# Position taps of the second pass in halves of two rows, two taps scaled by ScalarE and summed by transfers, queries of two groups in quarters

## The chip, the cores and the metric

The kernel runs on one core of a Trainium2 chip. The metric is the device time of one execution in microseconds (us), the median of several runs. The engines are named as in the profile: PE (TensorE, matmuls), PEld (its weight loads), DVE (VectorE), ACT (ScalarE), POOL (GpSimd) and SP (SyncE, which here only issues transfers).

## What is computed

The input x has 4 images of 192 channels and 128 x 128 pixels, in float32. Two layers follow one another:

```python
# layer 0: 1x1 convolution to q, k, v, l, a 3x3 convolution of each channel,
# attention between the 24 channels of a head, a gate from l, projection
# layer 1:
pe = depthwise_conv3x3(x, pos_w)                       # padding 1
x = x + pe + pos_b
q, k, v = split(einsum('oc,bchw->bohw', qkv_w, x))     # three groups of 64 channels each
for dil in (1, 2, 3):                                  # one group each, two heads of 32 channels
    # each pixel attends to the 3x3 pixels around it at distance dil (reflected at the edges)
    scores = sum_d(q * k_at_9_pixels) / sqrt(32); a = softmax(scores); o = sum_9(a * v_at_9_pixels)
out = einsum('oc,bchw->bohw', proj_w, concatenate(o))
```

The change lies in layer 1, in the step `x + pe + pos_b` and in the product that makes q.

## The kernel before, in words

Three stages run one after the other: `project` (1x1 and 3x3 convolutions of layer 0), `channel_attention`, and `second_pass`, which holds the end of layer 0 and all of layer 1. The second pass treats two images at a time in blocks of RB = 4 rows (512 pixels): 64 blocks, n = 0 to 63, the first 32 for images 0 and 1. A block goes through these steps.

- **h**: transfers load x and the values of layer 0 (`loads`, SP's queue, buffers `xv`); PE multiplies (`h_product`, L870), ACT adds the gate and writes the rows into rings of 12 rows (`h_evict`, L874). Channels 0 to 127 of the two images lie side by side in `hboth`; channels 128 to 191 of both images share the partitions of a third ring.
- **y**, the nine position taps, for channels 0 to 127 of two images, 1024 elements in each of 128 partitions: ACT starts the sum in PSUM with the centre tap and the bias (`centre`, L910), seven taps follow on DVE, each a multiply and add into the same sum (`tap`, L922; the last writes to y in SBUF). ACT scales the ninth tap (`moved`, L934) and POOL adds it (`moved_sum`, L939). For channels 128 to 191, ACT scales all nine taps (`side`, L946), two accumulating transfers that POOL issues sum rows of three taps (`side_rows`, L958), and POOL adds the remaining three (`side_sum`, L966 and L969).
- **k, v**: PE multiplies y (`kv_product`, L1009, L1012), ACT copies the result into rings (`kv_evict`, L1022).
- **q and scores**: `query` makes q of one group in a PSUM bank: two products of 64 columns for y's first 128 channels (L1069), one full product for the rest (L1066). DVE multiplies q with three shifted windows of k at a time (`prod`, L1077, nine a block), PE sums over a head's channels (`pick_sums`, L1088).
- **softmax**: a transposing product by a constant `order` (L1137), then DVE, ACT and POOL in turn (L1140 to L1170), and a transposing transfer.
- **output**: PE spreads each weight over its channels (`expand`, L1210, 27 a block), DVE multiplies with a window of v (`term`, L1216, 27 a block), POOL sums them (`term_sum`, L1219, 24 a block), PE projects (`out_product`, L1228, L1232), ACT evicts and SP stores.

**What sets the order.** Each step is added to a planner (`Schedule.add`) with its engine, a rank, a cost in us, and the steps that it comes after. The planner plays the steps through: whenever an engine is free, it takes the step of lowest rank of those ready, and writes down the order. A change of tiling mode on PE is charged, and counts against a step's rank. The instructions are issued in this order, and each engine works through its own list in order. A rank is n plus a number of the table `PLACES`, plus a step for each repeat. Buffers take part: `hold` makes the first step of a use wait for the last step of the use that had the buffer before. [...] `pc` 2, `ex` 2, `q` 1, `sc` 1, and `pa`, the sum of the taps, one buffer of two banks.

Of the kernel before, what the change touches and what calls it, by code (L numbers as in the profile page):

```python
# [9 lines left out]
AF = mybir.ActivationFunctionType  # L10
# [176 lines left out]
def rows3(t):  # L187
    return t.rearrange("p (r w) -> p r w", w=W)


FULL, COLS, ROWS, QUADS = "128x128", "128x64", "64x128", "128x32"
HALVES = [slice(0, G), slice(G, 128)]
EXTRA = 2 * B * CH0 + B
SM = EXTRA + B * 2 * CH0
XV = 8
GATE = "wl wl2 dwl fc1T bfc1 fc2T bfc2 eye wprojT".split()
SECOND = "wp1 wq1 wq2 wkv wkv2 wo wo2 posw posb pick order spread".split()
AROUND = (0, 1, 2, 6, 7, 8, 3, 5)

PLACES = {
    "loads": (2.4009, 0),
    "h_product0": (2.3439, 0),
    "h_evict0": (-1.2020, 0),
    "h_product1": (2.8426, 0),
    "h_evict1": (9.5243, 0),
    "h_product2": (3.0534, 0),
    "h_evict2": (3.3755, 0),  # L210
    "centre": (3.2944, 0),
    "tap": (4.7047, 0),
    "moved": (5.7274, 0),
    "moved_sum0": (8.4467, 0),
    "side1": (2.5636, 0.00009),
    "side0": (4.2983, 0.34214),
    "side_rows0": (4.7711, 0),
    "side2": (4.3133, 0),
    "side_rows2": (4.5576, 0),
    "side_sum1": (12.0962, 0),  # L220
    "side_sum2": (7.0378, 0),
    "kv0": (5.2031, 0),
    "kvev0": (3.8148, 0),
    "kv1": (6.4619, 0),
    "kvev1": (8.5235, 0.00001),
    "kv2": (6.0990, 0.18519),
    "kvev2": (5.9292, 0),
    "query0": (6.1573, 0.00001),
    "prod0": (6.9366, 0.00008),
    "query1": (6.5060, 0),  # L230
    "prod1": (7.1376, 0),
    "query2": (7.1323, 0.00003),
    "prod2": (7.5724, 0.00451),
    "pick0": (4.7039, 0.95999),
    "pick1": (15.4739, 0),
    "evicted_scores": (8.2142, 0),
    "by_pixel": (4.8132, 0),
    "top": (9.2303, 0),
    "below": (13.5404, 0),
    "exponential": (4.7718, 0),  # L240
    "total": (6.8232, 0),
    "divide": (3.7907, 0),
    "part0": (4.5732, 0),
    "rest": (6.0317, 0),
    "part1": (5.9516, 0),
    "part2": (6.6828, 0),
    "weights": (7.4677, 0),
    "expand": (8.0527, 0.03805),
    "term": (7.9973, 0),
    "term_sum": (9.4625, 0.01039),  # L250
    "out0": (9.2437, 0),
    "outev0": (9.1400, 0),
    "store0": (7.8234, 0),
    "out1": (9.4456, 0.00001),
    "outev1": (9.8720, 0),
    "store1": (8.3096, 0),
}

@with_exitstack
# [549 lines left out]
def second_pass(tc, x, w2, xv_p, mix1, mix2, biases, v_dram, v2_dram, out):  # L809
# [4 lines left out]
    with ExitStack() as ctx:  # L814
# [5 lines left out]
            dict(  # L820
                xv=XV, y=3, y2=3, prod=4, middle=2, side=1, moved=1, term=4, acc=4, o=3, s_sb=1, e=2, mx=2, sm=2, e_sb=2,
            ),
            dict(pc=2, ex=2, q=1, pa=1, sc=1),
            dict(xv=xv_p),
            (0.12, 0.4177),
        )
        add, hold, tile_of, tiles = stage.schedule.add, stage.hold, stage.tile, stage.tiles
        fill, read, repeat, written = stage.fill, stage.read, stage.repeat, stage.written
# [14 lines left out]
        def at(name, n, k=0):  # L843
            first, step = PLACES[name]
            return n + first + step * k
# [57 lines left out]


        by_row = lambda a: a.rearrange("p r b w -> p (r b) w")

        def centre(n):
            at = n * RB % RING
            to, of = tile_of("pa", ("pa", n), (128, RB, 2, W)), hboth[:, at : at + RB, :, 1 : W + 1]
            nc.scalar.activation(  # L910
                by_row(to), by_row(of), AF.Identity, bias=posb[:, 0:1], scale=posw[:, 0, 4:5]
            )

        def tap(n, t, last):

            acc = tiles["pa", n]
            to = tile_of("y", ("y", n), (128, RB, 2, W)) if last else acc
            if last:
                for im in range(2):
                    tiles["y", n, im] = to[:, :, im, :]  # L920
            for at, length, o in runs(n, t // 3 - 1, RING, False):
                nc.vector.scalar_tensor_tensor(  # L922
                    by_row(to[:, o : o + length]),
                    by_row(hboth[:, at : at + length, :, t % 3 : t % 3 + W]),
                    posw[:, 0, t : t + 1],
                    by_row(acc[:, o : o + length]),
                    ALU.mult,
                    ALU.add,
                )

        def moved(n, t):
            to = tile_of("moved", ("moved", n), (128, RB, 2, W))
            at = n * RB % RING
            nc.scalar.activation(  # L934
                by_row(to), by_row(hboth[:, at : at + RB, :, t % 3 : t % 3 + W]), AF.Copy, scale=posw[:, 0, t : t + 1]
            )

        def moved_sum(n):
            nc.gpsimd.tensor_add(tiles["y", n], tiles["y", n], tiles.pop(("moved", n)))  # L939

        def side(n, ty, tx):

# [19 lines left out]
        def side_sum(n, tx):  # L962
# [5 lines left out]
            y = tiles["y", n, 2]  # L968
            nc.gpsimd.tensor_add(y, y, tiles.pop(("side", n, 1))[:, 2, :])  # L969

        def plan_conv(n):
            prev = first = add("ACT", at("centre", n), 1.25, (centre, n), latency=0.3)
            for m in range(2):
                read("h", m, n, 0, first)
            for j, t in enumerate(AROUND[:7]):
                prev = add("DVE", at("tap", n, j), 1.19, (tap, n, t, j == 6), [prev])
                for m in range(2):
                    read("h", m, n, t // 3 - 1, prev)
            hold("pa", first, prev)
            two = prev  # L980
            mv = add("ACT", at("moved", n), 1.2, (moved, n, AROUND[7]))
            for m in range(2):
                read("h", m, n, 0, mv)
            both = add("POOL", at("moved_sum0", n), 2.39, (moved_sum, n), [mv, two])
            hold("moved", mv, both)
            firsts, sums = {}, []
            for j, ty in enumerate((1, 0, 2)):
                for tx in range(3):
                    sd = add("ACT", at(f"side{ty}", n, tx), 0.72, (side, n, ty, tx), firsts.get(ty, [])[-1:])
                    read("h", 2, n, ty - 1, sd)  # L990
                    firsts.setdefault(ty, []).append(sd)
                if j:
                    after = [firsts[1][-1], firsts[ty][-1], *sums[-1:]]
                    sums.append(add("POOL", at(f"side_rows{ty}", n), 0.9, (side_rows, n, ty), after, latency=6.0))
                    hold("side", firsts[ty][0], sums[-1])
            for tx in (1, 2):
                sums.append(add("POOL", at(f"side_sum{tx}", n), 1.26, (side_sum, n, tx), sums[-1:]))
            hold("middle", firsts[1][0], sums[-1])
            return [sums[-2], two, both, [both, sums[-1]]]


        def kv_product(n, pair, j):
# [16 lines left out]
        def kv_evict(n, pair, im, e, kind, g):  # L1019

            _, _, rows, pad = ring_rows(n, kind, g)
            nc.scalar.copy(rows[HALVES[im], :, pad : pad + W], rows3(tiles["pkv", n, pair, im])[HALVES[e]])  # L1022

        def reflect(n, kind, g):
            _, _, rows, pad = ring_rows(n, kind, g)
# [33 lines left out]
            for at, length, o in runs(n, dy, size, True):  # L1059
                yield ring[g][:, at : at + length, dx : dx + W], slice(o * W, (o + length) * W)  # L1060

        def query(n, g, j):

            q = tile_of("q", ("q", n, g)) if j == 0 else tiles["q", n, g]
            if j:
                mm(q, wq2[:, g, :], tiles["y", n, 2], start=False, stop=True)  # L1066
                return
            for im in range(2):
                mm(rows3(q[HALVES[im]]), wq1[:, g * G : (g + 1) * G], tiles["y", n, im], start=True, stop=False)  # L1069

        def prod(n, g, ty):

# [22 lines left out]

        def plan_scores(n, y):
            prods, used, picks = [], [], []
            for g in range(NG):
                a = add("PE", at(f"query{g}", n), 1.0, (query, n, g, 0), [y[2]], COLS)
                b = add("PE", at(f"query{g}", n, 1), 0.86, (query, n, g, 1), [a] + y[3], FULL)  # L1100
                used += [a, b]
                mine = []
                for ty in range(3):
                    op = add("DVE", at(f"prod{g}", n, ty), 1.67, (prod, n, g, ty), [b])
                    read("k", g, n, (ty - 1) * (g + 1), op)
                    mine.append(op)
                hold("q", a, *mine)
                prods += mine
            for row in range(7):
                of = prods[4 * row // 3 : min(4 * row + 3, NG * NT - 1) // 3 + 1]  # L1110
                op = add("PE", at(f"pick{row % 2 * (row < 6)}", n, row // 2), 0.86, (pick_sums, n, row), of, QUADS)
                op["after"] += picks[-1:]
                picks.append(op)
            for k, op in enumerate(prods):
                hold("prod", op, picks[(3 * k + 2) // 4])
            return used, picks
# [183 lines left out]
def _shapes_only():  # L1300
# [6 lines left out]
    pick[np.arange(128), QR + np.arange(128) // HD1] = 1  # L1307
    order = np.zeros((128, NS), f)
    for col in range(NS):
        order[col // 4 % 4 * 32 + col // 16 * 4 + col % 4, col] = 1  # L1310
    spread = np.zeros((3, NT, 4, NT, 4, HD1), f)
    for t in range(NT):
        for h in range(4):
# [117 lines left out]
```

## Time and profile before

| | |
|---|---|
| median of 3 runs | 4451.89 us (4449.25 to 4452.1) |
| profiled execution | 4448.27 us |
| its span, first to last instruction | 4446.5 us |
| instructions | 64145 |
| mean granted TensorE clock | 0.987 of full speed |
| busy share of the span: PE, DVE, ACT, POOL | 98%, 87%, 57%, 75% |
| transfers | 608.93 MB, of it 99.89 MB on the queue of POOL |
| first centre tap of the second pass | 1644.3 us |
| last tap | starts at 4254.8 us |

A row of the profile names the line of the kernel, the engine, the operation, what it writes and reads (buffer numbers left out), the shape as partitions x elements, and the number of instructions; behind the first bar stand the busy time in us and the mean length of one in ns, behind the second the idle time before them and what ended it. [...] what an instruction costs is read from its start to the next start. In the rows of waits, the first name had to wait for the second: us in total, times, longest.

### The profile page before, as it was taken

The page shows a single profiled execution, that of the slowest core. Times are in us where ns is not written, and L with a number is a line of the kernel's source. Part 1 is how long each engine was busy: PE and PEld are TensorE (multiplying, and loading weights), DVE is VectorE, ACT ScalarE, POOL GpSimd, SP SyncE. Part 2 cuts the span into 40 slices and gives each one's busy share as a digit, 9 for nine tenths or more (in the row PEclk, how much of TensorE's full clock was granted, in tenths as well). Part 3 has the DMA queues.
Part 4 walks back from the last instruction along what each step waited for, and adds up shares of the span by engine and source line. Part 5 has one row for each costly group of instructions (what it writes and reads, how often), then busy time and mean ns, then how long its engine had stood idle before and what let it go on. Part 6 is the DMA issues. An engine that isn't in the chain of part 4 may idle for free.

```text
span 4446.5 us, 64145 instructions
## 1 busy us (share of the span) xinstructions
PE 4340.2 (98%) x20608; PEld 1632.8 (37%) x20608; DVE 3875.7 (87%) x5556; ACT 2523.0 (57%) x4794; POOL 3350.1 (75%) x3343
## 2 busy tenths in 40 slices
PE   9999999899999998999999999999999999999996
PEld 3333333354455542333333333333333333333321
DVE  7998888855555546999999999999999999999996
ACT  7888888733333336555556555555555555555531
POOL 6787777711211113999999999999999999999998
PEclk9999999999999999999999999999999999999997
DMA  8777787678876744444444444444444444443411
GB/s 270 243 246 230 239 255 245 197 163 177 181 170 141 172 104 114 109 98 107 103 104 103 100 103 111 104 100 102 96 104 104 99 111 99 110 105 93 98 36 32
DMA packets 483951, 608.93 MB, mean 137 GB/s; under 512 B 136528, under 2 KB 318364, under 8 KB 483616
## 3 DMA queue, kind: packets, MB, share of 16 engines
q1 hardware_dynamic: 464160, 504.94, 42.0%
q0 software_dynamic: 19456, 99.89, 11.4%
q8 instruction: 166, 2.72, 0.3%
q14 instruction: 169, 1.38, 0.1%
HBM read 277.72 MB, written 201.33 MB: 108 GB/s over the span
## 4 chain that ended last, share of the span: by engine, by line
PE 92%; POOL 3%; DVE 2%; DMA 1%; issue 1%; ACT 1%; SPq 0%; POOLq 0%; DVEq 0%; ACTq 0%
PE pc L638 11%; PE ph L870 11%; PE sc L1088 9%; PE ex L1210 9%; PE pu L355 7%; PE pkv L1009 7%; PE pkv L1012 4%; PE pu L360 4%; PE gram L710 4%; PE q L1069 4%; PE po L1232 4%; PE po L1228 4%; PE q L1066 4%; PE pu L488 2%; POOL acc L1219 2%; PE pu L369 1%
## 5 line engine op out<-in xcount | busy, mean ns | idle before, releaser
L1219 POOL TENSOR_TENSOR acc<-acc,term 128x512 f32<-128x512 f32 x1536 | 1984.4, 1297 | 101.7 <-DVE term L1216 34.4
L1216 DVE TENSOR_TENSOR term<-ex,vring 128x512 f32<-128x512 f32 (+2 forms) x1596 | 1001.9, 666 | 29.2 <-PE ex L1210 18.8
L1077 DVE TENSOR_TENSOR prod<-q,kring 128x1536 f32<-128x1536 f32 (+1 forms) x600 | 1005.7, 1690 | 19.3 <-ACT kring L1027 11.0
L425 POOL TENSOR_TENSOR v_True<-v_True,side 128x512 f32<-128x512 f32 (+1 forms) x512 | 647.8, 1267 | 171.2 <-ACT side L414 143.7
L402 DVE SCALAR_TENSOR_TENSOR pa<-vboth,dwv,pa 128x1024 f32<-128x1024 f32 (+1 forms) x448 | 574.3, 1282 | 78.4 <-ACT pa L395 55.7
L1210 PE MATMUL ex<-e_sb,spread 108*128 108x512 bf16 x1728 | 556.8, 387 | 28.0 <-DVE term L1216 22.1
L922 DVE SCALAR_TENSOR_TENSOR pa<-hboth,posw,pa 128x1024 f32<-128x1024 f32 (+1 forms) x384 | 492.0, 1281 | 34.0 <-ACT pa L910 20.7
L625 POOL COPY band<-band 64x384 f32<-64x384 f32 x192 | 96.6, 503 | 560.9 <-DMA band<-in_bands 392.1
L638 PE MATMUL pc<-u,band 64*64 64x508 f32 (+1 forms) x4608 | 516.9, 590 | 1.5 <-ACT ring L384 1.5
L1088 PE MATMUL sc<-prod,pick 128*32 128x512 f32 x3456 | 475.1, 604 | 2.3 <-DVE prod L1077 1.5
L651 DVE BATCH_NORM_STATS2 stats<-pc 128x6 f32<-128x128 f32 x1440 | 303.3, 284 | 140.8 <-ACT conv L647 140.6
L1009 PE MATMUL pkv<-y,wkv 128*128 128x512 f32 x768 | 371.6, 605 | 11.1 <-ACT vring L1022 10.8
L647 ACT COPY conv<-pc 128x512 f32<-128x512 f32 x384 | 211.5, 587 | 294.7 <-PE pc L638 288.1
L355 PE MATMUL pu<-xt,wx 128*128 128x512 f32 x768 | 366.4, 613 | 8.5 <-DMA xt<-in_x 8.5
L870 PE MATMUL ph<-xv,mix 128*128 128x512 f32 (+1 forms) x1024 | 369.2, 597 | 3.0 <-DMA xv<-v_dram 2.4
L414 ACT ACTIVATE side<-ring,dwv 128x512 f32<-128x512 f32 (+1 forms) x512 | 350.7, 736 | 11.6 <-POOL v_True L425 10.9
L1210 PEld LDWEIGHTS <-spread 108*128 108x128 bf16 x1728 | 130.3, 98 | 610.7 <-issue 592.7
L1022 ACT COPY kring<-pkv 64x512 f32<-64x512 f32 x384 | 223.6, 582 | 228.5 <-PE pkv L1012 223.0
L946 ACT ACTIVATE side<-hring,posw 128x512 f32<-128x512 f32 x512 | 338.6, 708 | 23.6 <-DMA side<-side 11.3
L1022 ACT COPY vring<-pkv 64x512 f32<-64x512 f32 x384 | 224.1, 583 | 136.5 <-PE pkv L1012 118.7
L638 PEld LDWEIGHTS pc<-u,band 64*64 64x64 f32 x4608 | 188.3, 133 | 301.8 <-issue 281.1
L373 ACT COPY us<-pu 128x512 f32<-128x512 f32 x384 | 203.7, 601 | 81.4 <-PE pu L360 81.4
(164 smaller groups left out, 5912.1 us busy)
## 6 DMA issues: line engine op xcount, KB each, us to landing
qk_dram<-us SPq DMA_DIRECT2D x192, 512.0 KB
u<-qk_dram SPq DMA_DIRECT2D x384, 256.0 KB
side<-side POOLq DMA_DIRECT2D x124, 768.0 KB, 6.3
xt<-in_x SPq DMA_DIRECT2D x64, 512.0 KB
v_dram<-v_False SPq DMA_DIRECT2D x64, 512.0 KB
xv<-in_x SPq DMA_DIRECT2D x128, 256.0 KB
xv<-v_dram SPq DMA_DIRECT2D x128, 256.0 KB
out<-o SPq DMA_DIRECT2D x128, 256.0 KB
```

What stands on the lines that cost most here:

```text
L355: mm(pu, wx[:, mt * 128 : (mt + 1) * 128], tiles["xt", n][:, im, :], start=True, stop=False)
L402: nc.vector.scalar_tensor_tensor(by_row(to[:, o : o + length]), by_row(vboth[:, at : at + length, :, t % 3 : t % 3 + W]), dwv[:, 0, t : t ...
L425: nc.gpsimd.tensor_add(v[:, rows, :], v[:, rows, :], z[:, rows, :])
L638: nc.tensor.matmul(pcs[e][r * G : (r + 1) * G, :, to], band[at, e, c, dx, :], u[at, e, c, :].rearrange("p (b w) -> p b w", w=W)[:, :, of], ...
L870: mm(to, w[:, cols], tiles["xv", n, j, im], start=j == 0, stop=j == 2)
L922: nc.vector.scalar_tensor_tensor(by_row(to[:, o : o + length]), by_row(hboth[:, at : at + length, :, t % 3 : t % 3 + W]), posw[:, 0, t : t ...
L1009: mm(rows3(tile_of("pc", key)), w, tiles["y", n, im], start=True, stop=False)
L1077: nc.vector.tensor_mul(to[:, :, px].rearrange("p t (r w) -> p t r w", w=W), q.unsqueeze(1).to_broadcast([128, 3, *q.shape[1:]]), three,)
L1088: mm(sc[quad * 32 : (quad + 1) * 32, :], pick[:, QR - 4 * row : QR - 4 * row + 32], tiles["prod", n, k // NT, k % NT // 3][:, k % 3, :], s ...
L1210: mm(rows3(tile_of("ex", ("ex", n, g, t))), spread[:, t, :], e_sb, start=True, stop=True)
L1216: nc.vector.tensor_mul(rows3(to[:, px]), rows3(ex[:, px]), win)
L1219: nc.gpsimd.tensor_add(tiles["acc", n, g], tiles["acc", n, g], tiles.pop(("term", n, g, t)))
```

## The change

**Position taps.** The sum of the taps now takes one bank: a half of two rows (512 elements) at a time, in the one buffer of `pa`. ACT starts a half (`centre`), DVE adds six taps to it (`tap`, taps 0, 1, 2, 6, 7, 5), then the next half follows. Taps 3 and 8 are both scaled by ACT into one tile (`moved`). Two accumulating transfers, issued by POOL, take the place of POOL's sum: the first adds the two scaled taps, the second adds their sum to y.

**Queries.** `q` has two buffers. The queries of groups 0 and 1 are made together: four products of 64 columns for the first 128 channels, and for the rest four products of 64 x 64, one in each quarter of the array, where there were two full ones. For that, group 1 has its two images in the other halves of the partitions (`place`), in q and in the ring of k, and the constant `order` is changed to match.

**Planner.** Accumulating transfers become two steps: an issue of 0.9 us on POOL and a transfer on an engine "DMA" of its own. All ranks in `PLACES` are new, and a change of tiling mode counts 0.1456 instead of 0.4177 against a rank.

```diff
+SUMMED, MOVED = (0, 1, 2, 6, 7, 5), (3, 8)
...
-    "loads": (2.4009, 0),
+    "loads": (-9.1531, 0),
-    "centre": (3.2944, 0),
-    "tap": (4.7047, 0),
-    "moved": (5.7274, 0),
-    "moved_sum0": (8.4467, 0),
+    "centre0": (1.7649, 0),
+    "tap0": (4.0491, 0),
+    "centre1": (2.2535, 0),
+    "tap1": (0.2255, 0.00005),
+    "moved": (5.4417, 0.00002),
+    "moved_sum0": (-1.3279, 0),
+    "moved_sum1": (2.2850, 0),
-    "prod0": (6.9366, 0.00008),
+    "prod0": (2.7121, 0.00004),
-    "prod2": (7.5724, 0.00451),
+    "prod2": (3.0588, 0.00004),
-    "term": (7.9973, 0),
+    "term": (4.3386, 0),
...
-            dict(pc=2, ex=2, q=1, pa=1, sc=1),
+            dict(pc=2, ex=2, q=2, pa=1, sc=1),
-            (0.12, 0.4177),
+            (0.12, 0.1456),
...
-        def centre(n):
+        place = lambda im, g, kind="k": HALVES[im ^ (g == SWAPPED and kind == "k")]
+        def centre(n, half):
+            at = (n * RB + 2 * half) % RING
+            to, of = tile_of("pa", ("pa", n, half), (128, 2, 2, W)), hboth[:, at : at + 2, :, 1 : W + 1]
...
-        def moved_sum(n):
-            nc.gpsimd.tensor_add(tiles["y", n], tiles["y", n], tiles.pop(("moved", n)))
+        def moved_sum(n, k):
+            reach = runs(n, MOVED[1 - k] // 3 - 1, RING, False)
+            flat = lambda a: a[:, reach[0][2] : reach[-1][2] + reach[-1][1]].rearrange("p r b w -> p (r b w)")
+            of = tiles["moved", n]
+            nc.gpsimd.dma_start(flat(tiles["y", n] if k else of[:, 0]), flat(of[:, 1 - k]), accum_op=ALU.add)
...
+        def summed_by_transfer(rank, us, run, after):
+            issue = add("POOL", rank, 0.9, run, after)
+            return add("DMA", rank + 0.01, us, (lambda: None,), [issue], latency=2.0)
...
-            prev = first = add("ACT", at("centre", n), 1.25, (centre, n), latency=0.3)
-            for j, t in enumerate(AROUND[:7]):
-                prev = add("DVE", at("tap", n, j), 1.19, (tap, n, t, j == 6), [prev])
-            mv = add("ACT", at("moved", n), 1.2, (moved, n, AROUND[7]))
-            both = add("POOL", at("moved_sum0", n), 2.39, (moved_sum, n), [mv, two])
+            for half in range(2):
+                prev = first = add("ACT", at(f"centre{half}", n), 0.68, (centre, n, half), two[-1:], latency=0.3)
+                for j, t in enumerate(SUMMED):
+                    u = at(f"tap{half}", n, j)
+                    prev = add("DVE", u, 0.62, (tap, n, t, half, j == 5), [prev])
+                hold("pa", first, prev)
+                two.append(prev)
+            for k, t in enumerate(MOVED):
+                mvs.append(add("ACT", at("moved", n, k), 1.15, (moved, n, k, t), mvs[-1:]))
+            both = summed_by_transfer(at("moved_sum0", n), 4.0, (moved_sum, n, 0), mvs)
+            both = summed_by_transfer(at("moved_sum1", n), 4.0, (moved_sum, n, 1), [both, two])
...
-                mm(q, wq2[:, g, :], tiles["y", n, 2], start=False, stop=True)
+                        w, of = wq2[HALVES[im], g, HALVES[im]], tiles["y", n, 2][HALVES[im]]
+                        mm(q[place(im, g)], w, of, start=False, stop=True)
...
-            for g in range(NG):
-                a = add("PE", at(f"query{g}", n), 1.0, (query, n, g, 0), [y[2]], COLS)
+            for groups in ((0, 1), (2,)):
+                a = add("PE", at(name, n), 1.0 * len(groups), (query, n, groups, 0), [y[2]], COLS)
+                second = QUARTERS if len(groups) == 2 else FULL
...
-        order[col // 4 % 4 * 32 + col // 16 * 4 + col % 4, col] = 1
+        head = col % 4 ^ 2 * (col // GT == SWAPPED)
+        order[col // 4 % 4 * 32 + col // 16 * 4 + head, col] = 1
```

## The prediction

> **What bounds the kernel now.** I read the page first. Its 40 slices show three stretches; the edit touches only the last one, the second pass, from about 1645 us (first centre tap) to the end. So the next view is the busy time of each engine in stretches of 420 us, ten blocks each, and in what follows the last tap at 4255 us.
>
> ```profile
> core 0: us, PE busy (x) PEld busy (x) DVE busy (x) ACT busy (x) POOL busy (x), PEclk, DMA share, GB/s
> 2100.00:2520.00 420.00, 420.00 (x1731) 144.22 (x1729) 418.96 (x471) 236.70 (x474) 395.85 (x320) 1.00 0.44 104
> 2520.00:2940.00 420.00, 418.37 (x1718) 143.87 (x1720) 416.50 (x468) 237.81 (x477) 395.16 (x319) 1.00 0.43 102
> 4255.00:4446.00 191.00, 149.35 (x537) 45.03 (x533) 142.69 (x203) 37.23 (x85) 167.21 (x135) 0.85 0.13 34
> ```
>
> PE, DVE and POOL all look full. A busy share can't part them, because matmul ends are modelled. Who waits for whom can; these are waits between 2000 and 4000 us (some 47.6 blocks), in us, times and the longest:
>
> ```profile
> PEld q L1069 <- DVE prod L1077: 40.3, 48, 1.1
> PEld sc L1088 <- DVE e L1144: 35.0, 46, 0.8
> POOL acc L1219 <- DVE term L1216: 24.2, 51, 0.7
> DVE term L1216 <- PE ex L1210: 1.4, 3, 0.6
> ```
>
> PE and POOL wait for DVE; DVE hardly waits for anyone. So DVE is the bound, and the sum of its instructions should give the length of a block. The maximum of the softmax runs once a block; ten of them start between 2121.0 and 2499.2 us, so a block takes 378.2/9 = **42.02 us**.
>
> ```profile
> L1140 DVE TENSOR_REDUCE mx<-st x10: 604/621/623, 2121.0 to 2499.2; 128x48 f32<-128x432 f32 x10
> ```
>
> The order of DVE's instructions in time gives what each costs from its start to the next start (first column start, second length of the group):
>
> ```profile
> 3017.14 2.61 DVE L922 SCALAR_TENSOR_TENSOR pa<-hboth,posw,pa 128x1024 f32<-128x1024 f32 x2
> 3019.66 0.68 DVE L1216 TENSOR_TENSOR acc<-ex,vring 128x512 f32<-128x512 f32 x1
> 3020.26 0.68 DVE L1216 TENSOR_TENSOR term<-ex,vring 128x512 f32<-128x512 f32 x1
> 3020.86 1.28 DVE L922 SCALAR_TENSOR_TENSOR pa<-hboth,posw,pa 128x1024 f32<-128x1024 f32 x1
> 3022.05 1.28 DVE L1216 TENSOR_TENSOR term<-ex,vring 128x512 f32<-128x512 f32 x2
> 3023.24 1.75 DVE L1077 TENSOR_TENSOR prod<-q,kring 128x1536 f32<-128x1536 f32 x1
> 3024.91 1.28 DVE L1216 TENSOR_TENSOR term<-ex,vring 128x512 f32<-128x512 f32 x2
> ```
>
> A product costs 1.67 (3023.24 to 3024.91), two terms 1.19 (3022.05 to 3023.24), a tap followed by other work 1.19 (3020.86 to 3022.05). Two taps in a row cost 2.52 (3017.14 to 3019.66), so a tap right behind the one whose sum it reads costs 0.13 more than 1.19: its predecessor has to be written out first. The softmax's four are 0.66 + 0.52 + 0.97 + 0.37 = 2.52 in the same view. Seven taps with on average 0.9 direct followers (57 of 448, counted in the trace) are 7 x 1.19 + 0.9 x 0.13 = 8.45. Block: 27 x 0.595 + 9 x 1.67 + 8.45 + 2.52 = 42.07, against 42.02 measured. The sum closes: **DVE is saturated**, and only its own sum, or a new wait, can move a block.
>
> [...] the tap of a border block, with 768 elements, is 270 ns shorter than one with 1024[...] the trace has 4608 matmuls of 64x64 in 516.9 us, 0.112 each. [...]
>
> **The change, part by part, for a block of four rows.**
>
> *DVE taps.* Seven of 1024 elements go, twelve of 512 come (six for each half). No row shows a 512-element tap, so I extrapolate:
>
> ```profile
> L922 DVE SCALAR_TENSOR_TENSOR pa<-hboth,posw,pa 128x1024 f32<-128x1024 f32 x372 | 479.7, 1290 | 25.3 <-ACT pa L910 12.1 <-ACT hboth L874 7.7 <-ACT hboth L175 2.9
> L922 DVE SCALAR_TENSOR_TENSOR pa<-hboth,posw,pa 128x768 f32<-128x768 f32 x12 | 12.2, 1020 | 8.8 <-ACT pa L910 8.7
> ```
>
> 1290 - 2 x 270 = 750 ns long; less the 0.10 by which a tap overlaps the next instruction (1.29 to 1.19), **0.65 us**, or 0.78 right behind its predecessor. Bounds: 0.60, what the cheapest 512-element operation here (a term) costs, and 0.78. The new planner figure is 0.62 (1.19 for the whole tap before); it has no price for a direct follower. Both rows span two banks, so a cost of crossing a bank, if there is one, would be in my 0.65. With k direct followers a block: 12 x 0.65 + 0.13 k = 7.80 + 0.13 k, against 8.45: **break-even at k = 5**. One tap fewer is worth no more than five extra fixed costs.
>
> *How many followers.* Half 0 has rank n + 4.05, behind most products and near terms (n + 4.34), so it fills gaps; half 1 has n + 0.23. In the kernel before the taps of block n run some 4.7 blocks ahead of the terms and 3 ahead of the products that run beside them (centre of the 31st block at 2821.1, its term work from 3019.7). At a lead of four a term has n - 4 + 4.34 = n + 0.34, behind half 1. So half 1 mostly runs as one burst: 5 followers. Half 0 goes into gaps between pairs of terms, where one whole tap went before and two halves fit: about 2. **k = 7**: 8.71, so +0.26 a block. With 62 of the 64 blocks in the saturated stretch: +16 us.
>
> *ACT.* One centre of 1.21 becomes two of 512 elements (0.7 to 0.8 each, side taps of 512 take 0.71 to 0.80), and one more scaled tap of 1.15 comes: about +1.4 a block. ACT is busy 237 of 420; what hides it is that DVE doesn't wait for ACT now. New wait: the centre of half 1 waits for the last tap of half 0, since one bank is left for these sums. Behind it on ACT stand evictions of h, keys and values; PE and the rings wait for those, and DVE for both. If DVE's order has no other work there, it costs up to a centre and two hand-overs, about 1 us; bounds 0 and 1, I take 0, since terms and products stand ready at most times.
>
> *POOL.* The sum of 1024 elements (2.36, or 2.32 start to start) goes; two accumulating transfers come. One such issue takes 0.61 until the next start and the next sum is 0.3 longer: 0.92. Its block was 24 x 1.277 + 2.32 + 1.23 + 1.24 + 2.85 (softmax) + 2 x 0.92 = 40.1 and becomes 39.7: still under DVE. Both issues wait in POOL's order, the first for the two scaled taps, the second for the first transfer and half 1; queued behind are term sums, and DVE needs their buffers (four terms, 5.1 us of cover). Landing at 512 KB: 576 KB took 5.6 and 768 KB 6.3, so about 5.4, twice in a row; before, the same sum took 2.4. Y is three deep and leads by blocks, so I cost that at nothing in the steady stretch and at 0 to 8 us once at the start.
>
> *DMA.* 128 x 512 KB more, 67 MB. The software queue's 99.9 MB took 11.4%; so 7.7% of the span, 13% of the pass: share 0.44 to 0.57. No bound.
>
> *PE.* The second half of two queries in quarters: eight quarter passes at 0.112 = 0.90 instead of four whole ones (four whole passes of the keys take 1.72 from their start to the next group's, 3018.92 to 3020.64 in PE's order): 1.72. PE gains 0.8 and the second query buffer frees it from waiting for products (40.3 us above). Since DVE waits for PE 1.4 us in 2000, this is worth nothing now: bounds 0 and 0.03 us a block. If the quarters don't overlap, it costs 0.8 on an engine with some 2 us of waits on DVE in each block.
>
> *Order and SP.* All places move. DVE's instructions other than taps are the same in number and size. Loads move to n - 9.15, so SP asks as early as eight buffers allow; a load that waits there holds the stores and the transpose behind it. With DVE the bound, cover is plenty. The stretch after the last tap (191 us, DVE 143 busy, POOL 167) may change by some 10 us either way; I take 0.
>
> *Sum.* The profiled execution took 4448.27 (span 4446.5), the median of the runs is 4451.89, 0.1% more. 4448.3 + 16 = **4464 us**. A measurement of this kernel can tell about 0.2% (9 us) from no change.
>
> **Rivals.** *Interleaved, or cheaper halves* (ends faster). The mechanism: the order puts terms between most taps (k = 3), or a sum in one bank costs the planner's 0.62. k = 3 at 0.65: 8.19, -0.26, so 4432. k = 3 at 0.62: 7.83, -0.62, so 4410. It decides from k below 5 at 0.65, or below 7.8 at 0.62. For it: taps before stand singly; a second query buffer gives DVE more choice. Against: half 1's rank. *A new wait on DVE*: between the halves, or for a term buffer that POOL frees late while it waits for a transfer. At 0.6 us a block on top: 42.9, +53, so about 4500. For it: four issues instead of two on POOL's queue in order, and one bank. Against: DVE waits were 0 in the steady stretch. *No change*: k near 5, or the drain gives back the 16: 4450. *The quarters don't run side by side*: PE is hidden anyway, as above, and the time is the forecast's.
>
> **How the numbers follow.** Forecast 0.46 (its own range 4455 to 4485), faster rival 0.27, new wait 0.17, no change 0.10. The range reaches to 4412 and 4500, leaving out the cheapest end of the faster rival and half of the wait's case. Faster than 4443: the rival and a sliver, 0.28. Within 0.2%: the fourth case and the low end of the forecast, 0.20. Slower: 0.52.
>
> **What would show it.** Half taps some 750 ns long and 0.65 to the next start; more than five a block directly behind one another; mean distance of the softmax maxima near 42.3; DVE without waits; PE and POOL with more waits on DVE. I am wrong if halves are near 0.62 and singled out by terms (41.4 a block), or if DVE shows waits for ACT or POOL in the steady stretch.

## The result, and the profile after

| | before | changed |
|---|---|---|
| median of 12 runs each | 4450.8 us | 4453.06 us |
| ratio to before, 95% interval | | 1.0005, 0.9996 to 1.0014 |
| span of the profiled execution | 4446.5 us | 4451.2 us |
| block of four rows in the steady stretch | 42.02 us | 42.11 us |

The change makes no difference that this measurement can tell. The prediction had the time 11 us too long. It held a slower kernel for likeliest (0.52), which didn't come, and gave this outcome 0.20; its range, 4412 to 4500 us, holds the time.

The rows that answer to those shown of before come from the same views. Busy time of each engine in ten blocks, twice, and after the last taps:

```profile
core 0: us, PE busy (x) PEld busy (x) DVE busy (x) ACT busy (x) POOL busy (x), PEclk, DMA share, GB/s
2100.00:2520.00 420.00, 414.38 (x1765) 137.82 (x1758) 417.54 (x521) 247.25 (x495) 390.22 (x331) 1.00 0.57 127
2520.00:2940.00 420.00, 414.88 (x1770) 138.01 (x1768) 417.14 (x520) 248.83 (x500) 391.80 (x331) 1.00 0.57 128
4255.00:4446.00 191.00, 152.65 (x541) 41.97 (x539) 144.74 (x207) 33.96 (x76) 168.94 (x137) 0.84 0.13 35
```

PE and POOL each have 3.4 to 5.6 us less work in 420, ACT has 10 to 11 more, the DMA share went from 0.44 to 0.57, and DVE is as full as before, with 50 instructions more. The last stretch changed by 2 us on DVE and POOL. The waits say the same:

```profile
POOL acc L1257 <- DVE term L1254: 67.5, 149, 1.5
DVE term L1254 <- PE ex L1248: 0.4, 1, 0.4
```

The second row is the only wait of DVE between 2000 and 4000 us that the view lists. POOL's wait for DVE's terms grew from 24.2 to 67.5: what POOL was spared became idle time. The softmax maxima give the block, (2503.0 - 2124.0)/9 = 42.11 us:

```profile
L1178 DVE TENSOR_REDUCE mx<-st x10: 594/594/598, 2124.0 to 2503.0; 128x48 f32<-128x432 f32 x10
```

The half taps, by shape (busy us, mean ns), and three places of DVE's order in one block of the steady stretch:

```profile
L931 DVE SCALAR_TENSOR_TENSOR pa<-hboth,posw,pa 128x512 f32<-128x512 f32 x630 | 469.8, 746 | 31.6 <-ACT pa L916 24.1
```

```profile
2129.51 0.75 DVE L931 SCALAR_TENSOR_TENSOR pa<-hboth,posw,pa 128x512 f32<-128x512 f32 x1
2130.29 0.75 DVE L931 SCALAR_TENSOR_TENSOR y<-hboth,posw,pa 128x512 f32<-128x512 f32 x1
...
2143.60 1.53 DVE L931 SCALAR_TENSOR_TENSOR pa<-hboth,posw,pa 128x512 f32<-128x512 f32 x2
2145.04 0.68 DVE L1254 TENSOR_TENSOR term<-ex,vring 128x512 f32<-128x512 f32 x1
2145.64 1.75 DVE L1113 TENSOR_TENSOR prod<-q,kring 128x1536 f32<-128x1536 f32 x1
2147.30 2.33 DVE L931 SCALAR_TENSOR_TENSOR pa<-hboth,posw,pa 128x512 f32<-128x512 f32 x3
2149.67 0.75 DVE L931 SCALAR_TENSOR_TENSOR y<-hboth,posw,pa 128x512 f32<-128x512 f32 x1
2150.33 0.68 DVE L1254 TENSOR_TENSOR acc<-ex,vring 128x512 f32<-128x512 f32 x1
...
2161.78 0.74 DVE L931 SCALAR_TENSOR_TENSOR pa<-hboth,posw,pa 128x512 f32<-128x512 f32 x1
2162.43 0.68 DVE L1254 TENSOR_TENSOR term<-ex,vring 128x512 f32<-128x512 f32 x1
2163.03 0.74 DVE L931 SCALAR_TENSOR_TENSOR pa<-hboth,posw,pa 128x512 f32<-128x512 f32 x1
```

The first two rows are the end of a half 0; the next taps are the half 1 behind it, and the last rows begin the next half 0. Half 1 comes almost as the burst that the ranks promised, in a pair and a four with a term and a product between them: four of its taps follow another tap directly, at 0.78 to 0.79 from start to start. Half 0 stands singly between other work, 0.65 to the next start, but for its last two taps. So a block of the steady stretch has 5 direct followers, 4 of half 1 and 1 of half 0. Over the whole pass 338 of 768 taps follow one of the same sum, 5.3 a block; the difference lies at the ends of the pass.

### The profile page after: what moved, and what is told of

The parts are those of the page before. It is cut to its first block, busy times and chain, and to the rows that moved or that the text cites. A ratio compares the mean times of both kernels' runs of the same rounds, so it can differ in the third digit from the quotient of the medians.

```text
span 4451.2 us, 65440 instructions
## 1 busy us (share of the span) xinstructions
PE 4312.1 (97%) x20864; PEld 1594.0 (36%) x20864; DVE 3870.5 (87%) x5876; ACT 2593.4 (58%) x4922; POOL 3320.8 (75%) x3407
## 3 DMA queue, kind: packets, MB, share of 16 engines
q14 instruction: 175, 1.43, 0.1%
## 4 chain that ended last, share of the span: by engine, by line
PE 76%; DVE 14%; issue 6%; POOL 2%; DMA 1%; ACT 1%; SPq 0%; POOLq 0%; DVEq 0%; ACTq 0%
PE pc L642 11%; PE sc L1124 9%; DVE term L1254 8%; PE pu L359 7%; PE pkv L1038 7%; PE ex L1248 7%; PE pkv L1041 4%; PE pu L364 4%; PE ph L874 4%; PE gram L714 4%; PE q L1102 4%; PE po L1270 4%; PE pu L492 2%; DVE pa L931 2%; DVE prod L1113 2%
## 5 line engine op out<-in xcount | busy, mean ns | idle before, releaser
L1257 POOL TENSOR_TENSOR acc<-acc,term 128x512 f32<-128x512 f32 x1536 | 2019.4, 1317 | 167.4 <-DVE term L1254 90.6
L1113 DVE TENSOR_TENSOR prod<-q,kring 128x1536 f32<-128x1536 f32 (+1 forms) x600 | 1001.2, 1681 | 21.3 <-PE q L1105 13.8
L1248 PE MATMUL ex<-e_sb,spread 108*128 108x512 bf16 x1728 | 604.2, 386 | 62.7 <-DVE term L1254 37.7
L931 DVE SCALAR_TENSOR_TENSOR pa<-hboth,posw,pa 128x512 f32<-128x512 f32 (+1 forms) x640 | 474.7, 742 | 39.7 <-ACT pa L916 32.1
L1124 PE MATMUL sc<-prod,pick 128*32 128x512 f32 x3456 | 447.2, 601 | 5.8 <-DVE e L1182 3.2
L874 PE MATMUL ph<-xv,mix 128*128 128x512 f32 (+1 forms) x1024 | 397.4, 602 | 5.3 <-DMA xv<-v_dram 4.7
L1248 PEld LDWEIGHTS <-spread 108*128 108x128 bf16 x1728 | 141.9, 97 | 653.2 <-issue 631.0
L963 ACT ACTIVATE side<-hring,posw 128x512 f32<-128x512 f32 (+1 forms) x512 | 334.4, 708 | 4.8 <-DMA side<-side 2.8
L1273 ACT COPY o<-po 128x512 f32<-128x512 f32 x192 | 106.3, 588 | 276.7 <-PE po L1266 185.9
```

Source lines behind the costliest of these rows:

```text
L874: mm(to, w[:, cols], tiles["xv", n, j, im], start=j == 0, stop=j == 2)
L931: nc.vector.scalar_tensor_tensor(by_row(to[:, o : o + length]), by_row(hboth[:, at : at + length, :, t % 3 : t % 3 + W]), posw[:, 0, t : t ...
L1113: nc.vector.tensor_mul(to[:, :, px].rearrange("p t (r w) -> p t r w", w=W), q.unsqueeze(1).to_broadcast([128, 3, *q.shape[1:]]), three,)
L1124: mm(sc[quad * 32 : (quad + 1) * 32, :], pick[:, QR - 4 * row : QR - 4 * row + 32], tiles["prod", n, k // NT, k % NT // 3][:, k % 3, :], s ...
L1248: mm(rows3(tile_of("ex", ("ex", n, g, t))), spread[:, t, :], e_sb, start=True, stop=True)
L1257: nc.gpsimd.tensor_add(tiles["acc", n, g], tiles["acc", n, g], tiles.pop(("term", n, g, t)))
```

## The experiments

**Theory A**: DVE is saturated; a block is 33.57 us (42.02 - 8.45) plus the taps, and what PE and POOL are spared is hidden. **Rivals**: the halves did free DVE and new waits took it back (B); PE (D) or POOL (E) binds beside DVE; the transfers slow the other engines (F). In each sum below the followers are those of the steady stretch, counted in the kernel's trace. Where an experiment "keeps the order", only what a step issues is changed, not the plan. All ratios are to the kernel before, run beside it on the same chip.

**What PE and POOL were spared is given back.** First the quarters:

```diff
-SWAPPED = 1
+SWAPPED = -1
...
-                if j and len(groups) == 1:
+                if j:
```

> The changed kernel with its order kept, but the second half of the queries of groups 0 and 1 made by two full products each in place of four quarters; the images keep their own halves of the partitions. PE gets about 0.8 us more a block. Theory A: PE's saving was hidden, so giving it back changes the time by less than 9 us. Rival D, PE is a bound beside DVE and the quarters paid for other losses: 30 to 50 us longer.

Measured: 4456.02 us, ratio 1.0010 (1.0002 to 1.0018), 3 us from the changed kernel. PE's busy time between 2100 and 2520 us rose from 414.38 to 418.33, 0.4 a block where 0.8 was expected:

```profile
2100.00:2520.00 420.00, 418.33 (x1722) 142.32 (x1713) 417.28 (x520) 246.57 (x495) 389.71 (x330) 1.00 0.57 128
```

Then the second transfer:

```diff
+            if k:
+                nc.gpsimd.tensor_add(flat(tiles["y", n]), flat(tiles["y", n]), flat(of[:, 0]))
+                return
```

> The changed kernel with its order kept, but the second accumulating transfer is a POOL sum of 1024 elements in the same place: POOL gets about 2.32 - 0.95 = 1.4 us more a block and one transfer fewer. Theory A: POOL has some 3 us of waits a block, so the time changes by less than 9 us. Rival E, POOL is a bound beside DVE: 40 us or more longer. Rival F, the transfers slow DVE, ACT or PE: it gets shorter by more than 9 us.

Measured: 4452.01 us, ratio 1.0001 (0.9993 to 1.0009). POOL's busy time rose by 14.4 us in ten blocks, 1.4 a block, and the block stayed at (2501.6 - 2122.6)/9 = 42.11:

```profile
2100.00:2520.00 420.00, 414.39 (x1766) 137.85 (x1762) 417.55 (x520) 246.89 (x495) 404.65 (x330) 1.00 0.49 115
```

D, E and F fall: both savings were hidden, and giving up one of the two transfers didn't shorten anything. The second query buffer stayed in both kernels; what it alone does was not measured.

**DVE gets less.** One tap is left out of each half:

```diff
         def tap(n, t, half, last):
+            if t == 0:
+                return
```

> The changed kernel with its order kept, and tap 0 left out of both halves (so that tap's part of the sum is missing): two DVE instructions fewer in a block. Theory A, DVE's own sum is the block: it goes by 0.656 in half 0 and 0.656 + 0.127 in the burst of half 1, 1.44 us a block, 62 blocks, down to 89 us less (about 4364), at least 35 us less if another engine binds soon. Rival B, the halves did free DVE and new waits on ACT, POOL or the transfers hold the block at 42.1: the time stays within 9 us of 4453 and DVE gets 1.4 us of waits a block.

Measured: 4402.18 us, ratio 0.9890 (0.9876 to 0.9903), 51 us less than the changed kernel. B falls: time follows DVE. But a block took (2529.2 - 2116.6)/10 = 41.26 us, not the 40.64 that the sum gives with its four followers (10 x 0.656 + 4 x 0.127 = 7.07). The trace shows what holds it: DVE's terms now wait for PE's `ex`. The wait between 2000 and 4000 us, and one place where it comes:

```profile
DVE term L1256 <- PE ex L1250: 9.1, 46, 0.5
```

```profile
2136.21 0.74 DVE L933 SCALAR_TENSOR_TENSOR pa<-hboth,posw,pa 128x512 f32<-128x512 f32 x1
2137.14 0.69 DVE L1256 TENSOR_TENSOR term<-ex,vring 128x512 f32<-128x512 f32 x1 [0.19 <-PE ex L1250]
```

Here the tap takes 0.93 to the next start instead of 0.66. Summed from start to start between 2100 and 2940 us, such delays come to 0.54 us a block, most of the missing 0.62. Whether PE is full in this kernel or the kept order only places `ex` too late was not separated.

**DVE gets more instructions.** Each half tap is issued row by row:

```diff
+                    for r in range(length):
...
-                        by_row(to[:, o : o + length]),
...
+                            by_row(to[:, o + r : o + r + 1]),
...
```

> The changed kernel with its order kept, but each half tap is two instructions of one row (256 elements) each: the fixed cost of an instruction is paid 24 times in a block instead of 12. Theory A, each instruction has a fixed 0.12 us on top of its elements: 0.39 us for each of 24, and no follower pays 0.13, since the piece in front is another row; 24 x 0.39 = 9.36 instead of 12 x 0.656 + 5.3 x 0.127 = 8.54, so +0.8 us a block, about 50 us longer (4503). Rival B, DVE has room beside another bound: less than 15 us longer.

Measured: 4622.05 us, ratio 1.0385 (1.0370 to 1.0399): 169 us longer, not 50. The fixed cost was right (a piece takes 0.397 to the next start, 0.39 was expected), the followers were not. DVE's order in time:

```profile
2516.33 1.01 DVE L932 SCALAR_TENSOR_TENSOR pa<-hboth,posw,pa 128x256 f32<-128x256 f32 x2
2517.25 0.94 DVE L1190 TENSOR_REDUCE sm<-e 128x48 f32<-128x432 f32 x1
...
2520.77 0.87 DVE L932 SCALAR_TENSOR_TENSOR y<-hboth,posw,pa 128x256 f32<-128x256 f32 x2
2521.55 1.28 DVE L1255 TENSOR_TENSOR term<-ex,vring 128x512 f32<-128x512 f32 x2
```

Two pieces that write the sum take 1.01 (0.52 from start to start), though they touch different rows; two that write y take 0.87 (0.40). The first kind carries a wait for DVE's own semaphore before its second piece, in all 630 such pairs of this kernel, and the second kind in none of 128. In the changed kernel's trace 337 of the 338 direct followers carry that wait; they start 0.78 after their predecessor's start and 0.035 after its recorded end (medians), where other work starts 0.655 after a tap's start. So a follower pays 0.13 because it waits for its predecessor to complete, and the program puts that wait between any two pieces that write this sum, whichever rows they touch. With 24 pieces at 0.397 and 15 such waits at 0.127 a block, the taps take 11.43 and a block 45.00; measured, (2514.0 - 2109.7)/9 = 44.92. Rival B falls once more.

**Whole taps, with the sum in SBUF.** Six taps of 1024 elements stand where half 0's stood (half 1 issues nothing, the output tiles have two buffers):

```diff
-... moved=1, term=4, acc=4, o=3, ...
+... moved=1, pa=1, term=4, acc=4, o=2, ...
-            dict(pc=2, ex=2, q=2, pa=1, sc=1),
+            dict(pc=2, ex=2, q=2, sc=1),
...
+            if half:
+                return
...
```

> The changed kernel with its order kept, but the sum of the taps lies in SBUF, whole: six taps of 1024 elements stand where half 0's taps stood, half 1's steps issue nothing. (The output tiles get two buffers instead of three, to make room.) Theory A: taps cost 6 x 1.19 = 7.14 instead of 12 x 0.656 + 5.3 x 0.127 = 8.54; 1.4 us a block, 50 to 87 us less than 4453, if a tap that reads its sum from SBUF costs what one from PSUM costs. Rival B: no gain, as above. Rival C: two operands in SBUF slow the taps or POOL's sums beside them; then L931 is longer than 1.29 or the POOL sums longer than 1.32, and the gain is under 35 us.

Measured: 4877.44 us, ratio 1.0952 (1.0936 to 1.0969). C holds, and by more than it said. Taps by shape, between 2000 and 4400 us:

```profile
L936 DVE SCALAR_TENSOR_TENSOR pa<-hboth,posw,pa 128x1024 f32<-128x1024 f32 x236 | 466.0, 1975 | 0.0
```

1975 ns against 1290 with the sum in PSUM (the kernel before), and the POOL sums went from 1317 to 1436. This says nothing on splitting; it says what it is worth here that the sum lies in PSUM. Why both engines got slower was not isolated.

**Fewer followers.** The changed kernel's instructions, with places found by a search of mine in a planner that knows the two numbers:

```diff
-release(o, end + op["latency"] * (o["engine"] != engine))
+release(o, end + (op["latency"] if o["engine"] != engine else op.get("lag", 0.0)))
... (all of PLACES)
-            (0.12, 0.1456),
+            (0.12, 0.1885),
...
-                    prev = add("DVE", u, 0.62, (tap, n, t, half, j == 5), [prev])
+                    prev = add("DVE", u, 0.655, (tap, n, t, half, j == 5), [prev])
+                    prev["lag"] = 0.13
```

> The changed kernel's instructions, with an order found by a search of places in which the planner knows that a half tap takes 0.655 and that its direct follower starts 0.13 later: 0.86 direct followers a block instead of 5.3; 25.3 changes of tiling mode on PE a block instead of 22.4. Theory A: taps cost 12 x 0.656 + 0.86 x 0.127 = 7.98 instead of 8.54, 0.56 us a block, 62 blocks: up to 35 us less, about 4420 to 4430. Rival B, other waits hold the block: within 9 us of 4453, and DVE waits 0.5 us a block.

Measured: 4602.44 us, ratio 1.0347 (1.0328 to 1.0366). Neither theory had this. Undisturbed blocks took 41.3, near the 41.55 of A's sum, but others took up to 59. DVE's waits between 2000 and 4000 us:

```profile
DVE term L1255 <- PE ex L1249: 70.4, 38, 2.7
DVE acc L1255 <- PE ex L1249: 54.8, 10, 12.7
```

PE in turn waited for the transposing transfer of the weights:

```profile
PEld L1249 <- DMA e_sb<-parts: 116.1, 24, 15.6
PE ex L1249 <- DMA e_sb<-parts: 103.6, 22, 15.3
```

My first thought was that its reader stood too close (5 to 8 us after the issue). So the planner got 10 us for this transfer and 0.70 for the centre of a half, and two searches gave two orders:

> As the earlier kernel with followers priced, but the planner also gives the transposing transfer of the weights 10 us instead of 6 (there its first reader stood as little as 5 us behind the issue, and waited up to 21), and 0.70 for the centre of a half. The search found an order with 1.3 direct followers a block. Theory A: taps cost 12 x 0.656 + 1.3 x 0.127 = 8.04 instead of 8.54: 0.5 us a block, up to 31 us less than 4453, and undisturbed blocks of 41.6 us. Rival B, other waits hold the block (26 changes of tiling mode a block instead of 22.4, PE): 4444 or more.

> The same as the one with 1.3 followers, by a search from another start: 2.5 direct followers a block and 24.1 changes of tiling mode. Theory A: taps cost 12 x 0.656 + 2.5 x 0.127 = 8.19 instead of 8.54: 0.35 us a block, up to 22 us less than 4453, and more than the one with 1.3 followers. Rival B: no relation of the time to the followers; the one with fewer changes of tiling mode is the faster.

Measured: 4621.33 us, ratio 1.0357 (1.0311 to 1.0403), with 1.3 followers, and **4427.89 us**, ratio 0.9945 (0.9930 to 0.9960), with 2.5. The second is as A says. The 2.5 are an average over the pass; a steady block has 2, so the taps take 12 x 0.656 + 2 x 0.127 = 8.13 and a block 41.70; measured, (2489.6 - 2113.9)/9 = 41.74:

```profile
L1179 DVE TENSOR_REDUCE mx<-st x10: 607/610/615, 2113.9 to 2489.6; 128x48 f32<-128x432 f32 x10
```

The first waits again, and more for accumulating transfers (POOL 172.2 us, ACT 129.7) than for the transposing one (PE's weight loads 78.3). Its first reader of the weights starts 11 us or more after the issue, so the longer lead didn't help, and for that kernel the relation to the followers can't be read. In both slow kernels the long blocks are those where an accumulating transfer of the sides was issued close to the transposing one. Between 2000 and 4000 us, in the kernel with 0.86 followers, 15 of 23 blocks in which the two stand less than 1 us apart were over 44 us (from issue to issue), and none of 22 in which they stand further apart; in the kernel with 1.3, 17 of 30 and 1 of 14. So one step of the kernel with 0.86 was moved: the second accumulating transfer of the sides is issued one POOL sum later.

```diff
         self.span = max(free.values())
+        for op in [o for o in out if getattr(o["run"][0], "__name__", "") == "side_rows" and o["run"][2] == 2]:
+            i = out.index(op)
+            j = next(k for k in range(i + 1, len(out)) if out[k]["engine"] == "POOL")
+            out.insert(j, out.pop(i))
```

> The kernel with 0.86 followers a block (4602 us, blocks of 41.3 us with others of 46 to 59 among them) with one step of its order moved: the second accumulating transfer of the sides is issued one POOL sum (1.3 us) later. In that kernel the long blocks are those where this transfer was issued within 1 us of the transposing transfer of the weights; now the two stand about 2 us or more apart. Theory A: the long blocks go away and the taps' saving shows, 12 x 0.656 + 0.86 x 0.127 = 7.98 instead of 8.54: about 4415 to 4430. Rival B, the long blocks come from too little time for the transposing transfer (5 to 8 us to its first reader), wherever the other transfer stands: 4550 or more.

Measured: **4424.13 us**, ratio 0.9939 (0.9922 to 0.9955): 178 us off by 1.3 us of distance, with no two of these transfers closer than 1.4 us between 2000 and 4000 us. The lead of the transposing transfer is as short as before (about 5 to 8 us, but for one block), so that wasn't it. The waits of PE for it between 2000 and 4000 us:

```profile
PEld L1253 <- DMA e_sb<-parts: 3.6, 5, 1.3
PE ex L1253 <- DMA e_sb<-parts: 0.9, 2, 0.6
```

In the steady stretch only one block of nine has a follower, so a block is 33.57 + 7.87 + 0.01 = 41.45 by the sum; measured, (2504.2 - 2131.8)/9 = 41.38:

```profile
L1183 DVE TENSOR_REDUCE mx<-st x10: 593/597/598, 2131.8 to 2504.2; 128x48 f32<-128x432 f32 x10
```

Over 62 blocks, 0.73 less a block would be 45 us; the kernel is 29 us shorter than the changed one. The rest is lost outside the steady stretch, 9 us of it before the first maximum of the softmax (1760.8 us instead of 1751.4).

**One part of the change alone.** In the kernel before, six whole taps in two banks, and two scaled taps summed by two transfers; the queries stay. The order is new, and the planner prices accumulating transfers as in the changed kernel:

```diff
-            for j, t in enumerate(AROUND[:7]):
-                prev = add("DVE", at("tap", n, j), 1.19, (tap, n, t, j == 6), [prev])
+            for j, t in enumerate(SUMMED):
+                prev = add("DVE", at("tap", n, j), 1.19, (tap, n, t, j == 5), [prev])
+                prev["lag"] = 0.13
...
-            both = add("POOL", at("moved_sum0", n), 2.39, (moved_sum, n), [mv, two])
+            both = summed_by_transfer(at("moved_sum0", n), 4.0, (moved_sum, n, 0), mvs)
+            both = summed_by_transfer(at("moved_sum1", n), 4.0, (moved_sum, n, 1), [both, two])
```

> The kernel before with one part of the change alone: six whole taps in two banks, two taps scaled by ACT and summed by two transfers; queries as before in one bank. The order is found by the same search, with followers priced at 0.13 (1.2 a block). Theory A: taps cost 6 x 1.19 + 1.2 x 0.13 = 7.3 instead of 8.45, a block 40.9 if DVE alone decides, 70 us less than before; since PE keeps the full products, it may bind first, between 40.9 and 41.6: 4380 to 4425. Rival B: no gain, as the transfers or PE hold 42: 4440 to 4460.

> Six whole taps and two moved, queries as before, with the transposing transfer given 20 us in the planner and a fresh order (1.2 followers a block). The earlier one with the same instructions took 4403. Theory A: DVE's sum is 40.9 and the full products of PE hold the block at about 41.2, so 4395 to 4412.

> Control: the kernel before, instructions unchanged, with an order found by the same search with followers priced at 0.13 (1.3 a block, planner's count for the kernel before: 1.3). Theory A: DVE's sum is the same, so the time stays within 9 us of 4451. If a fresh search alone gains more than 9 us, the gains of the other two are not due to the taps alone.

Measured: 4403.28 us, ratio 0.9897 (0.9883 to 0.9910); with the second order **4389.43 us**, ratio 0.9861 (0.9846 to 0.9876), the fastest here; and the control 4437.12 us, ratio 0.9968 (0.9956 to 0.9981). The control misses its band by 5 us: a fresh search is worth 14 us, most of it at the start (92 us instead of 102 from the first tap to the first maximum of the softmax), for its steady blocks take 42.0 as before. The other two gain 48 and 61 us, and 28 and 45 of that lie between the first maximum and the last, where the control gains 1.5. For the fastest, (2517.5 - 2106.6)/10 = 41.09:

```profile
L1159 DVE TENSOR_REDUCE mx<-st x11: 602/604/606, 2106.6 to 2517.5; 128x48 f32<-128x432 f32 x11
```

For both the sum gives 33.57 + 6 x 1.19 + 1 x 0.13 = 40.84. The first one's block is 41.29: its terms wait for PE's `ex`, 18.7 us in 50 waits between 2000 and 4000 us. In the fastest one that wait is nearly gone (1.2 us), but once a block a term starts 1.43 after the tap in front of it instead of 1.19, and in 19 of 20 blocks it is a sum on POOL that releases it in the trace. These 0.24 are the whole difference:

```profile
2122.97 1.29 DVE L924 SCALAR_TENSOR_TENSOR pa<-hboth,posw,pa 128x1024 f32<-128x1024 f32 x1
2124.40 0.69 DVE L1235 TENSOR_TENSOR term<-ex,vring 128x512 f32<-128x512 f32 x1
```

## Why the prediction was right, and where not

- **DVE is the bound**: shown. Less on DVE shortens a block (41.26 us with a tap less, 42.11 in the changed kernel), more lengthens it (44.92 row by row). Where DVE has no regular wait (the sum in SBUF and the two slow orders apart), the sum holds within 0.1 us: 42.08 by the sum and 42.11 measured for the changed kernel, 45.00 and 44.92 row by row, 41.70 and 41.74, 41.45 and 41.38 with fewer followers. Where the sum falls below 41, a term waits once or more a block for PE or POOL, and the block is 0.25 to 0.6 longer than the sum (the kernel with a tap less and the two with whole taps).
- **A half tap takes 750 ns, 0.65 to the next start**: measured 746 and 0.656. The planner's 0.62 is 0.035 short. The figure came from taps over two banks (1290 and 1020 ns) and held for halves in one, so staying in one bank saved nothing that shows. A fixed cost of 0.12 us an instruction is an estimate from the times to the next start of a half and a whole tap, 2 x 0.656 - 1.19; what it consists of was not shown.
- **A follower pays 0.13**: measured 0.127 (0.783 against 0.656). The reason is sharper than I gave it: it is the wait for the predecessor's completion, in the kernel with single rows also where no data pass between them.
- **k = 7**: this is the term that was off. Both of its parts were one too high in the steady stretch: half 1 gives 4 followers, not 5, since a term and a product split it once, and half 0 gives 1, not 2, since terms come one at a time there and a half fits between two. So k is 5, the taps take 12 x 0.656 + 5 x 0.127 = 8.51, not 8.71, and a block 42.08 (measured 42.11), not 42.28; over 62 blocks the measured difference is 10 of the 11 us. Break-even was put at k = 5: the time is the "no change" case by that case's own cause. That it lies in the range says little, as the range also holds a gain of 39 us.
- **0.9 followers in the kernel before**: the count of 57 in 448 is too low. In its trace 83 taps follow one of the same sum directly, 1.3 a block. A steady block has 1, so the sum of 8.45 stands.
- **PE, POOL, ACT, DMA at nothing**: shown for POOL and for PE's quarters by giving the savings back. ACT's new wait between the halves didn't reach DVE in the steady stretch; over the whole pass DVE waited 32.1 us for centres, before 20.7. The DMA share came out at 0.57 as worked out.
- **Landing 5.4 us for 512 KB**: the medians were 4.5 and 4.6, and 768 KB went from 6.3 to 6.9. Taking one of the two away changed nothing (4452.01 us, and 4453.06 with both), so it didn't matter.
- **Halves that are singled out are faster**, the rival: true as a mechanism (steady blocks of 41.38 and 41.74 instead of 42.11), but the change's order didn't do it. That the times, 4424 and 4428, lie between its 4410 and 4432 is in part due to the fresh orders.
- **What I didn't think of**: that whole taps with the same two moved would gain most. The gain of the change, 1.19 us of DVE time for a tap less, was spent on six more instructions than six whole taps need (12 x 0.656 - 6 x 1.19 = 0.73) and four more followers a block (0.51).

## What to carry to other kernels

Add up the start-to-start times of the saturated engine before splitting its work: the fixed costs of more instructions at some 0.12 us each (estimated above), and direct followers at 0.13, ate what one tap less had saved. A planner that prices instructions without the wait between dependent neighbours has no reason not to put them in a row. Orders found with that number were 25 us faster in one case and 29 in another, there only after one transfer had been moved by hand; two such orders, this one before the move among them, lost some 150 and 170 us to transfers, and how much of the 25 and 29 a fresh search without the number would have found was not measured (in the kernel before, a fresh search gained 14). Moving work off the full engine without splitting the rest, in a fresh order, was worth 61. Look at the distance between the issues of a transposing and an accumulating transfer: below 1 us 32 of 53 blocks of two kernels took over 44 us, above it 1 of 36.

## What the runs showed of the hardware that was not expected

- A multiply-and-add on DVE with both operands in SBUF took 1975 ns on average for 1024 elements, against 1290 with one in PSUM, both while POOL sums in SBUF; the POOL sums beside it took 1436 on average, and 1317 in the changed kernel.
- In two kernels a transposing transfer and a 768 KB accumulating one were often issued less than 1 us apart (in 23 of 45 blocks and 30 of 44), and 15 and 17 of these blocks took over 44 us. Between 2000 and 4000 us, landings of the accumulating ones went up to 21.3 us in the kernel with 0.86 followers and 26.5 in the one with 1.3 (medians 6.3 and 7.0), and in the first PE waited up to 15.6 for the transposed weights. Moving one by 1.3 us ended it there (landings of at most 7.9). What in the transfers' path does this stays open.
